# Second graph-attention layer: stored sums, residual rows and small statistics moved to GpSimd, and an eighth closed in nine pieces, one per step

## The chip, the cores and the metric

The kernel runs on one core of a Trainium2 chip. The metric is the device time of one execution in microseconds, the median over several runs. A core has TensorE (PE in the profile; its weight loads are PEld), VectorE (DVE), ScalarE (ACT), GpSimd (POOL) and SyncE (SP), each with a queue of its own that it works off in order, and 16 DMA engines.

## The reference

Two graph-attention layers on the same graph of 4096 nodes, each with a residual and a layer norm:

```python
x = _layernorm(x + gat0(x, adj))   # 8 heads of 128, elu, then a product with W_out and b_out
x = _layernorm(x + gat1(x, adj))   # 4 heads of 64, heads side by side
```

In the second layer, for each head h:

```python
xt  = einsum('ni,hio->hno', x, W)
e   = leaky_relu(src[h, i] + dst[h, j], 0.2), minus infinity where adj[i, j] == 0
att = softmax(e, over j)
out[i, h] = sum over j of att[h, i, j] * xt[h, j]
```

The adjacency has about 32 neighbours a row, and the second layer works on the dense matrix.

## The kernel before, in words

**First layer** (from the start to about 1740 us). It makes lists of neighbours, gathers rows by indirect DMAs from GpSimd's queue (L975) and works through pairs of groups; the second layer's steps are mixed in as their inputs become ready.

**Second layer** (class `Dense`). The target nodes are cut into eight *eighths* of 512 columns, c = 0 to 7, the source nodes into 32 rows of 128, j. A *step* is one (c, j): an adjacency tile `aq` of 512 KB (for two steps) and projected rows `wh` are loaded by SP; ACT makes a mask `mb` of `aq` (L1279, for two steps); DVE makes four weights `e`, one for each head, 128x512 f32, out of `rb` and `mb`, two tiles in SBUF, and a scalar (L1288); PE multiplies them into three PSUM banks `po`, two with the weighted sums (L1312) and one with the denominators (L1322). The functions `load`, `mask`, `weigh` and `multiply` do that, and `ahead` keeps loads four steps, masks two and weights one ahead of the product. There are 14 buffers for `e`, 15 for the sums (pool `sum2`) and two sets of PSUM banks that take turns.

An eighth's steps become ready in *parts*, as the first layer gives rows. When a part that isn't an eighth's last ends, `evict` copies the three banks to SBUF by ACT (L1347) and stores them by ACT's DMA queue in `acc` (L1354). When a later part of the same eighth is to end, its last step's `load` fetches the stored sums back as `hs` (`held` in the code, L1270). PE then adds them into the banks by products with the identity (L1334), and `evict` copies the banks over `hs`.

After the first layer `depth` is 4. There, eighth 4 ends a part (stored once more) at 1898 us, eighth 6 one at about 1974 us, and then the last parts come in the order of c: eighths 0 to 6 with 8, 8, 4, 8, 4, 8 and 4 steps, each ending with stored sums, and eighth 7 with all its 32 steps and none stored.

**Closing of an eighth** (`unit1`). The eighth's last `evict` is followed by 13 pieces on the list `late`: sums of the denominators on PE (`dens`, tile `pd`, L1479), their inversion on DVE (`invert1`, L1488 and L1489), turns of the sums on PE (`turn`, tile `pt`, L1494), scaling on ACT (`share`, L1507), the residual add on DVE (`add`, L1514), means and spreads on ACT with accumulators (L1520, L1530), small 128x4 operations on DVE (`mean` L1524, `spread` L1540, `shift` L1547) and one power on GpSimd (L1541), the norm on ACT and the store of the output by SP (L1556). The order in which the pieces stand between the steps is written out by hand:

```python
while dense.more():
    if dense.weighed:
        dense.multiply()
    dense.ahead()
    late.some(2)
    while dense.ends:
        unit1(*dense.ends.pop(0))
late.all()
```

So after each step two pieces are issued, and every engine meets them in that order between its share of the steps.

Of the kernel before, what the change touches and what calls it, by code (L numbers as in the profile page):

```python
# [15 lines left out]
ALU = mybir.AluOpType  # L16
# [6 lines left out]
EPS = 1e-5  # L23
# [223 lines left out]
class Late:  # L247
# [5 lines left out]
    def add(self, *fs):  # L253
        self.items.extend(fs)
# [37 lines left out]
def fast_path(  # L292
# [11 lines left out]
    nc = tc.nc  # L304
    N, F = x.shape
# [76 lines left out]
    late, then, group, after = Lane(), Lane(), Lane(), Lane()  # L382
# [832 lines left out]
    class Dense:  # L1215
# [78 lines left out]
        def multiply(self):  # L1294
            s, es, wh = self.weighed.pop(0)
            part, j, start, stop = s
            c = part["c"]
            if start:
                self.n += 1
                sets = ((ps_d, "d0", 1), (ps_d, "d1", 1), (ps_d, "d2", 1))  # L1300
                if self.depth > 2 and self.n % 2:
                    sets = ((ps_o, "o0", 2), (ps_o, "o0", 2), (ps_o, "o1", 1))
                part["po"] = [
                    pool.tile([P, HB], F32, tag=tag, name=f"po_1_{c}_{j}_{q}", bufs=b)
                    for q, (pool, tag, b) in enumerate(sets)
                ]
            po = part["po"]
            held = part.get("held") if stop else None
            end = stop and not held
            for q in range(NQ):  # L1310
                for b in range(2 * D1 // DQ):
                    nc.tensor.matmul(  # L1312
                        po[q][ts(b, DQ), :],
                        wh[:, ds(q * 2 * D1 + b * DQ, DQ)],
                        es[2 * q + b * DQ // D1],
                        start=start,
                        stop=end,
                        tile_position=(0, b * DQ),
                        skip_group_check=True,
                    )  # L1320
            for h in range(H1):
                nc.tensor.matmul(  # L1322
                    po[NQ][ts(h, DQ), :],
                    sc1.cj[:, j, h : h + 1].to_broadcast([P, DQ]),
                    es[h],
                    start=start,
                    stop=end,
                    tile_position=(0, h * DQ),
                    skip_group_check=True,
                )  # L1330
            if stop:
                if held:
                    for t, p in zip(held, po):
                        nc.tensor.matmul(  # L1334
                            p, ident, t, start=False, stop=True, skip_group_check=True
                        )
                self.evict(part, held)

        def evict(self, part, hs):
            c = part["c"]  # L1340
            po = part.pop("po")
            hs = hs or [
                self.sum.tile([P, HB], F32, tag="h1", name=f"h_1_{c}_{part['e']}_{q}")
                for q in range(NQ + 1)
            ]
            for t, p in zip(hs, po):
                nc.scalar.copy(t, p)  # L1347
            if part["last"]:
                self.ends.append((c, hs))
                return  # L1350
            if c not in acc_d:
                acc_d[c] = dram.tile([NQ + 1, P, HB], F32, name=f"acc_{c}")
            for k, t in enumerate(hs):
                nc.scalar.dma_start(acc_d[c][k], t)  # L1354
# [114 lines left out]
    def unit1(c, hs):  # L1469
        i0 = c * CQ  # L1470
        rd = small.tile([P, nt, H1], F32, tag="rd", name=f"rd_{c}", bufs=2)
        y_sb = fin.tile([P, nt, F], F32, tag="y", name=f"y_{c}", bufs=6)
        nc.sync.dma_start(y_sb, x1_d[ts(c, HB), :].rearrange("(t p) f -> p t f", p=P))
        held = {}

        def dens():
            pt = held["d"] = ps_m.tile([P, nt, H1], F32, tag="m", name=f"pd_{c}")
            for k in range(nt):
                nc.tensor.matmul(  # L1479
                    pt[:, k],  # L1480
                    hs[NQ][:, ts(k, P)],
                    ident.rearrange("p (m d) -> p m d", d=DQ)[:, :, 0],
                    start=True,
                    stop=True,
                )

        def invert1():
            nc.vector.tensor_scalar(rd, held.pop("d"), NONE, None, ALU.max)  # L1488
            nc.vector.reciprocal(rd, rd)  # L1489

        def turn(q):
            pt = held[q] = ps_m.tile([P, nt, 2, D1], F32, tag="m", name=f"pt_{c}_{q}")
            for k in range(nt):
                nc.tensor.transpose(  # L1494
                    pt[:, k].rearrange("p a d -> p (a d)"), hs[q][:, ts(k, P)], ident
                )

        def share(q, half):
            if half == 0:
                held["z", q] = fin.tile(  # L1500
                    [P, nt, 2, D1], F32, tag="z", name=f"z_{c}_{q}", bufs=2
                )
            z, pt = held["z", q], held[q]
            for k in (2 * half, 2 * half + 1):
                for a in range(2):
                    h = 2 * q + a
                    nc.scalar.activation(  # L1507
                        z[:, k, a], pt[:, k, a], AF.Copy, scale=rd[:, k, h : h + 1]
                    )

        def add(q):
            z = held["z", q].rearrange("p k a d -> p k (a d)")
            y = y_sb[:, :, ts(q, 2 * D1)]
            nc.vector.tensor_tensor(y, y, z, ALU.add)  # L1514

        def means():
            st = held["st"] = small.tile([P, 3, nt], F32, tag="st1", name=f"st_1_{c}", bufs=2)
            for k in range(nt):
                o = fin.tile([P, F], F32, tag="o", name=f"o1_{c}_{k}")
                nc.scalar.activation(o, y_sb[:, k], AF.Copy, accum_out=st[:, 0, k : k + 1])  # L1520

        def mean():
            st = held["st"]
            nc.vector.tensor_scalar(st[:, 0], st[:, 0], -1.0 / F, None, ALU.mult)  # L1524

        def spreads():
            st = held["st"]
            for k in range(nt):
                o = fin.tile([P, F], F32, tag="o", name=f"o2_{c}_{k}")
                nc.scalar.activation(  # L1530
                    o,
                    y_sb[:, k],
                    AF.Square,
                    bias=st[:, 0, k : k + 1],
                    accum_out=st[:, 1, k : k + 1],
                )

        def spread():
            st = held["st"]
            nc.vector.tensor_scalar(st[:, 1], st[:, 1], 1.0 / F, EPS, ALU.mult, ALU.add)  # L1540
            nc.gpsimd.tensor_tensor(  # L1541
                st[:, 1], st[:, 1], neg_half.to_broadcast([P, nt]), ALU.pow
            )

        def shift():
            st = held["st"]
            nc.vector.tensor_tensor(st[:, 2], st[:, 0], st[:, 1], ALU.mult)  # L1547

        def norms():
            st = held["st"]  # L1550
            for k in range(nt):
                y = y_sb[:, k]
                nc.scalar.activation(
                    y, y, AF.Identity, scale=st[:, 1, k : k + 1], bias=st[:, 2, k : k + 1]
                )
            nc.sync.dma_start(out[ts(c, HB), :].rearrange("(t p) f -> p t f", p=P), y_sb)  # L1556

        late.add(
            dens,
            lambda: (invert1(), turn(0)),  # L1560
            lambda: share(0, 0),
            lambda: (share(0, 1), turn(1)),
            lambda: (add(0), share(1, 0)),
            lambda: share(1, 1),
            lambda: add(1),
            means,
            mean,
            spreads,
            spread,
            shift,  # L1570
            norms,
        )

# [16 lines left out]
    with tc.manual_schedule():  # L1590
        verdict()
        while dense.more():
            if dense.weighed:
                dense.multiply()
            dense.ahead()
            late.some(2)
            while dense.ends:
                unit1(*dense.ends.pop(0))
        late.all()
# [3 lines left out]
def kernel(  # L1603
# [21 lines left out]
    with ExitStack() as inner:  # L1625
        fast_path(
            inner, tc, flag_sb, x, xT, adj, adjT, w0f, w0T, a0, w_out, b_out, w1f, w1T, a1, out
        )
# [48 lines left out]
```

## Time and profile before

| | us |
|---|---|
| median of 9 runs (lowest to highest) | 2240.29 (2232.39 to 2245.64) |
| profiled execution, its own time | 2245.11 |
| its span | 2243.3 |
| PE busy (its share of the span) | 1624.5 (72%) |
| DVE busy | 1537.1 (69%) |
| POOL busy | 1173.3 (52%) |
| ACT busy | 813.8 (36%) |
| granted TensorE clock, mean | 0.877 |

The costs of operations in the stage from 1995 to 2132 us, by groups: an `e` 745 ns (consecutive ones overlap), an identity product 610 ns for each of its two passes, a copy of a bank 585 ns, a residual add on DVE 687 ns, a small 128x4 operation on DVE 162 to 169 ns, the power on POOL 1166 ns. PE's ends are modelled, so its busy share is not read as work; distances between starts are.

In the views below a line of a timeline has the start in us, the length in us, the engine, the line of the kernel, the operation, output and inputs by name, the number of instructions, and in brackets how long the engine had been idle before it and what ended that.

### The profile page before, as it was taken

The page shows a single profiled execution, that of the slowest core. Times are in us where ns is not written, and L with a number is a line of the kernel's source. Part 1 is how long each engine was busy: PE and PEld are TensorE (multiplying, and loading weights), DVE is VectorE, ACT ScalarE, POOL GpSimd, SP SyncE. Part 2 cuts the span into 40 slices and gives each one's busy share as a digit, 9 for nine tenths or more (in the row PEclk, how much of TensorE's full clock was granted, in tenths as well). Part 3 has the DMA queues.
Part 4 walks back from the last instruction along what each step waited for, and adds up shares of the span by engine and source line. Part 5 has one row for each costly group of instructions (what it writes and reads, how often), then busy time and mean ns, then how long its engine had stood idle before and what let it go on. Part 6 is the DMA issues. An engine that isn't in the chain of part 4 may idle for free. (4 is left out here: it accounts for less than half of the span.)

```text
span 2243.3 us, 34216 instructions
## 1 busy us (share of the span) xinstructions
PE 1624.5 (72%) x12092; PEld 845.2 (38%) x12092; DVE 1537.1 (69%) x3456; ACT 813.8 (36%) x1811; POOL 1173.3 (52%) x1189
## 2 busy tenths in 40 slices
PE   3414455556666753787599778788899989999996
PEld 2412333344343432544334334434444433333332
DVE  1533657646837836677687984978677677997896
ACT  3143433434434433434334424222233313235552
POOL 0056767777777777677677756766776000000000
PEclk9999667777887877697799988989999999999998
DMA  6888977857968957977878986655676337566651
GB/s 183 142 291 142 226 153 214 161 160 213 236 159 262 209 154 210 203 216 206 241 196 286 246 164 205 216 168 174 229 250 218 108 118 250 175 207 244 232 173 40
DMA packets 202259, 442.11 MB, mean 197 GB/s; under 512 B 52643, under 2 KB 76310, under 8 KB 199134
## 3 DMA queue, kind: packets, MB, share of 16 engines
q1 hardware_dynamic: 123790, 261.44, 36.5%
q0 software_dynamic: 55296, 161.10, 31.1%
q10 hardware_dynamic: 22992, 17.29, 2.4%
q8 instruction: 98, 1.61, 0.3%
q14 instruction: 83, 0.68, 0.1%
HBM read 414.81 MB, written 29.08 MB: 198 GB/s over the span
## 5 line engine op out<-in xcount | busy, mean ns | idle before, releaser
L975 POOL DMA_INDIRECT G<-table,ids x1152 | 1160.8, 1008 | 563.2 <-issue 301.7
L1288 DVE SCALAR_TENSOR_TENSOR e<-rb,pj,mb 128x512 f32<-128x512 f32 x1024 | 697.3, 749 | 116.3 <-PE po L1322 69.3
L1312 PE MATMUL po<-e,wh 128*32 128x512 f32 x4096 | 606.6, 628 | 98.5 <-DVE e L1288 98.5
L1322 PE MATMUL po<-e,cj 128*32 128x512 f32 x2048 | 344.1, 607 | 0.0
L1020 ACT ACTIVATE ag<-po,void 128x257 f32<-128x257 f32 x288 | 120.8, 471 | 528.2 <-PE pa L1037 503.5
L1312 PEld LDWEIGHTS po<-e,wh 128*32 128x32 f32 x4096 | 158.8, 112 | 395.7 <-DVE e L1288 237.8
L1069 PE MATMUL ph<-aT,w_sb 128*128 128x128 f32 x1152 | 185.3, 328 | 161.8 <-DVE hT L1083 151.4
L1541 POOL TENSOR_TENSOR st<-st,neg_half 128x4 f32<-128x4 f32 x8 | 9.2, 1152 | 495.6 <-DVE st L1540 495.6
L994 DVE TENSOR_TENSOR e<-rb,G 128x256 f32<-128x256 f32 x144 | 61.0, 423 | 281.8 <-DMA G<-table,ids 275.5
L1069 PEld LDWEIGHTS ph<-aT,w_sb 128*128 128x128 f32 x1152 | 174.8, 240 | 184.6 <-issue 111.9
L1010 PE MATMUL po<-G,e 128*32 128x257 f32 x2304 | 192.9, 450 | 63.8 <-DVE e L1001 28.5
L647 ACT ACTIVATE mb<-aq,less 114x1024 fp8e4<-114x1024 int32 x144 | 165.9, 1153 | 84.5 <-DMA aq<-in_adj 78.4
L1279 ACT ACTIVATE mb<-aq 128x1024 bf16<-128x1024 int32 x128 | 134.7, 1057 | 148.2 <-DVE e L1288 78.9
L1322 PEld LDWEIGHTS po<-e,cj 128*32 128x32 f32 x2048 | 97.1, 114 | 135.0 <-issue 110.9
L1090 PE MATMUL py<-wo_sb,hT 128*128 128x256 f32 x576 | 138.3, 396 | 5.6 <-DVE hT L1083 5.6
L1010 PEld LDWEIGHTS po<-G,e 128*32 128x32 f32 x2304 | 77.8, 123 | 132.1 <-issue 58.9
L1090 PEld LDWEIGHTS py<-wo_sb,hT 128*128 128x128 f32 x576 | 113.2, 202 | 22.5 <-DVE hT L1083 6.8
L1037 PE MATMUL pa<-ident,ag 128*128 128x128 f32 x576 | 109.5, 320 | 15.4 <-DVE pc L461 8.3
L1037 PEld LDWEIGHTS pa<-ident,ag 128*128 128x128 f32 x576 | 70.7, 159 | 114.1 <-issue 74.2
L1028 DVE TENSOR_TENSOR ag<-ag,rd_all 128x512 f32<-128x512 f32 x144 | 100.7, 699 | 8.9
L1039 ACT COPY aT<-pa 128x512 f32<-128x512 f32 x144 | 84.9, 589 | 18.8 <-DVE key L659 8.4
L1083 DVE SCALAR_TENSOR_TENSOR hT<-el,ph 128x512 f32<-128x512 f32 x72 | 48.2, 670 | 57.9 <-ACT el L1080 57.8
(182 smaller groups left out, 1590.3 us busy)
## 6 DMA issues: line engine op xcount, KB each, us to landing
aq<-in_adj SPq DMA_DIRECT2D x140, 512.0 KB
aq<-in_adjT SPq DMA_DIRECT2D x128, 512.0 KB
wh<-wh_d SPq DMA_DIRECT2D x128, 256.0 KB
rb<-r_d SPq DMA_DIRECT2D x23, 1024.0 KB
rb<-r_d SPq DMA_DIRECT2D x36, 512.0 KB
G<-table,ids POOLq DMA_INDIRECT x1152
hs<-acc SPq DMA_DIRECT2D x45, 256.0 KB
acc<-hs ACTq DMA_DIRECT2D x24, 256.0 KB
```

The source lines that it names most:

```text
L647: nc.scalar.activation(bins[m], raw.pop(m)[0:R], AF.Sign, bias=less[0:R], accum_out=held["deg"][:, t, q : q + 1], saturate=False,)
L975: nc.gpsimd.indirect_dma_start(out=G[:, b, :], out_offset=None, in_=table[:, :], in_offset=bass.IndirectOffsetOnAxis(ap=lists[s][0][:, c : ...
L1010: nc.tensor.matmul(po[ts(b, H0 * T), :], e[:, m * NB + b].rearrange("p h t -> p (h t)"), G[:, m * NB + b, 0 : F + 1], start=True, stop=Tru ...
L1020: nc.scalar.activation(ag[:, m], po, AF.Identity, bias=void[:, 0, v : v + 1])
L1028: nc.vector.tensor_tensor(ag[:, :, 0:F], ag[:, :, 0:F], rd.unsqueeze(2).to_broadcast([P, 2, F]), ALU.mult)
L1037: nc.tensor.transpose(pt[:, c, m], ag[:, m, ts(c, P)], ident)
L1069: nc.tensor.matmul(phs[k][:, hh, :], w_sb[:, c, ts(h, D0)], aT[:, c, h, :], start=(c == 0), stop=(c == KC - 1),)
L1090: nc.tensor.matmul(pys[0], hT[:, h, :], wo_sb[:, h, :], start=(h == 0), stop=(h == H0 - 1))
L1279: nc.scalar.activation(self.mb, aq, AF.Relu, scale=OPEN)
L1288: nc.vector.scalar_tensor_tensor(e, part["rb"][:, h], sc1.pj[:, j, h : h + 1], mb, ALU.max, ALU.min)
L1312: nc.tensor.matmul(po[q][ts(b, DQ), :], wh[:, ds(q * 2 * D1 + b * DQ, DQ)], es[2 * q + b * DQ // D1], start=start, stop=end, tile_position ...
L1322: nc.tensor.matmul(po[NQ][ts(h, DQ), :], sc1.cj[:, j, h : h + 1].to_broadcast([P, DQ]), es[h], start=start, stop=end, tile_position=(0, h ...
```

## The change

- In the stage after the first layer (`depth` above 2) stored sums are no longer added by PE. ACT copies the banks to three new tiles, and GpSimd adds `hs` to each. In the earlier stage PE still adds them.
- The three copies are made in reverse order everywhere, the denominators' first.
- The residual adds, `mean`, the first operation of `spread`, and `shift` go from DVE to GpSimd.
- The 13 pieces become nine: the denominators' sums with the first turn, the inversion by itself, the two halves of each scaling together, mean with spreads, spread with shift. One piece is issued per step, two while the list is longer than nine.

```diff
@@ multiply
-            end = stop and not held
+            end = stop and (not held or self.depth > 2)
...
             if stop:
-                if held:
+                if not end:
                     for t, p in zip(held, po):
                         nc.tensor.matmul(
                             p, ident, t, start=False, stop=True, skip_group_check=True
                         )
-                self.evict(part, held)
-
-        def evict(self, part, hs):
+                self.evict(part, held, end)
+
+        def evict(self, part, held, apart):
             c = part["c"]
             po = part.pop("po")
-            hs = hs or [
+            hs = held if held and not apart else [
                 self.sum.tile([P, HB], F32, tag="h1", name=f"h_1_{c}_{part['e']}_{q}")
                 for q in range(NQ + 1)
             ]
-            for t, p in zip(hs, po):
+            for t, p in zip(hs[::-1], po[::-1]):
                 nc.scalar.copy(t, p)
+            if held and apart:
+                for t, u in zip(hs[::-1], held[::-1]):
+                    nc.gpsimd.tensor_tensor(t, t, u, ALU.add)
@@ unit1: add, mean, spread, shift
-            nc.vector.tensor_tensor(y, y, z, ALU.add)
+            nc.gpsimd.tensor_tensor(y, y, z, ALU.add)
...
-            nc.vector.tensor_scalar(st[:, 0], st[:, 0], -1.0 / F, None, ALU.mult)
+            nc.gpsimd.tensor_scalar(st[:, 0], st[:, 0], -1.0 / F, None, ALU.mult)
...
-            nc.vector.tensor_scalar(st[:, 1], st[:, 1], 1.0 / F, EPS, ALU.mult, ALU.add)
+            nc.gpsimd.tensor_scalar(st[:, 1], st[:, 1], 1.0 / F, EPS, ALU.mult, ALU.add)
...
-            nc.vector.tensor_tensor(st[:, 2], st[:, 0], st[:, 1], ALU.mult)
+            nc.gpsimd.tensor_tensor(st[:, 2], st[:, 0], st[:, 1], ALU.mult)
@@ the pieces
-            dens,
-            lambda: (invert1(), turn(0)),
-            lambda: share(0, 0),
-            lambda: (share(0, 1), turn(1)),
-            lambda: (add(0), share(1, 0)),
-            lambda: share(1, 1),
+            lambda: (dens(), turn(0)),
+            invert1,
+            lambda: (share(0, 0), share(0, 1), turn(1)),
+            lambda: (add(0), share(1, 0), share(1, 1)),
             lambda: add(1),
             means,
-            mean,
-            spreads,
-            spread,
-            shift,
+            lambda: (mean(), spreads()),
+            lambda: (spread(), shift()),
             norms,
@@ the loop
-            late.some(2)
+            late.some(2 if len(late.items) > 9 else 1)
```

In the built program 24 products leave PE's queue, and GpSimd's gets 24 adds of stored sums, 16 residual adds and 24 small operations. In this queue the adds of an eighth's sums can stand ahead of the small operations of the eighth before it.

## The prediction

> **What bounds the kernel now.** I read the page's slices first, to find the stage that the change touches.
>
> ```profile
> PE   3414455556666753787599778788899989999996
> DVE  1533657646837836677687984978677677997896
> POOL 0056767777777777677677756766776000000000
> ```
>
> A slice is 56.1 us. POOL is empty from slice 32 (1740 us) on: the gathers are over and only second-layer steps run. Next I cut that stage in windows; the columns behind the window are its length and the busy time of PE, PEld, DVE, ACT and POOL.
>
> ```profile
> 1903.00:1998.00 95.00, 95.00 (x850) 37.13 (x842) 94.76 (x144) 20.67 (x23) 0.00 (x0) 1.00 0.63 210
> 1998.00:2165.00 167.00, 163.73 (x1283) 58.18 (x1284) 134.80 (x233) 96.71 (x291) 8.21 (x7) 1.00 0.59 204
> 2165.00:2220.00 55.00, 55.00 (x502) 22.67 (x498) 53.90 (x83) 11.96 (x14) 0.00 (x0) 1.00 0.36 121
> ```
>
> In the first and third window no eighth is closed and DVE never rests; in the middle one, where seven eighths end and are closed, it rests or does other things for a fifth of the time. So I took DVE's timeline there, around the closing of eighth 0.
>
> ```profile
> 1903.24 95.51 DVE L1288 SCALAR_TENSOR_TENSOR e<-rb,pj,mb 128x512 f32<-128x512 f32 x144 [0.41 <-ACT mb L1279]
> 2001.92 0.17 DVE L1488 TENSOR_SCALAR rd<-pd 128x16 f32<-128x16 f32 x1 [3.17 <-PE pd L1479]
> 2002.13 0.25 DVE L1489 RECIPROCAL rd<-rd 128x16 f32<-128x16 f32 x1
> 2002.30 5.30 DVE L1288 SCALAR_TENSOR_TENSOR e<-rb,pj,mb 128x512 f32<-128x512 f32 x8
> 2007.52 0.69 DVE L1514 TENSOR_TENSOR y<-y,z 128x512 f32<-128x512 f32 x1
> ...
> 2016.74 0.17 DVE L1540 TENSOR_SCALAR st<-st 128x4 f32<-128x4 f32 x1
> 2018.07 0.16 DVE L1547 TENSOR_TENSOR st<-st 128x4 f32<-128x4 f32 x1 [1.17 <-POOL st L1541]
> ```
>
> A weight e costs 95.51/144 = 0.663 us, a step (four) 2.65 us, and nothing on DVE comes between them except the closing, which DVE does in line and for which it waits (the brackets). Last, PE's timeline at the same place.
>
> ```profile
> 1995.35 2.84 PE L1334 MATMUL po<-hs,ident 128*128 128x512 f32 x6
> 1998.12 1.93 PE L1312 MATMUL po<-e,wh 128*32 128x512 f32 x16
> 2000.83 1.05 PE L1479 MATMUL pd<-ident,hs 128*128 128x4 f32 x8
> 2001.75 0.63 PE L1494 MATMUL pt<-ident,hs 128*128 128x128 f32 x4
> ```
>
> The identity products hold PE 2.77 us (1995.35 to 1998.12). An unhindered step takes 2.57 us (in the chain ten steps reach from 1903.42 to 1929.16, 2.574 each). Two steps with the sums and both turns of an eighth reach from 1998.12 to 2005.61, 7.49 us, so these cost 7.49 - 5.15 = 2.34 us.
>
> Two sums over the rest. **DVE**, from the last e of the 144 (1998.75) to the last e of all (2218.9): 220.1 us, of which 264 e make 175.0, waits 31.9 (the brackets added up) and closing work 13.2. **PE**, from 1995.35 to 2220.6, 225.3 us: 68 steps make 175.0, seven closings 16.4, seven identity products 19.4, together 210.8; it stands about 14. DVE is the bound, PE is close behind.
>
> **Removed.** In this stretch, 21 identity products leave PE (19.4 us), and 14 residual adds and 21 small operations leave DVE. What stays on DVE is the inversion of the denominators, 7 x (0.17 + 0.25) = 3.0 us. Its wait goes too: sums and turn now come a step before it, so PE has a whole step (2.57) to produce pd, where DVE waited 3.17 or 0.26. The waits on ACT and POOL leave DVE because POOL does those operations. DVE would then need 175.0 + 3.0 = 178.0 us, PE 210.8 - 19.4 = 191.4: if nothing else happened PE would be late next.
>
> **Added.** POOL gets, in this stretch, 21 adds of stored sums and 14 of residual rows, all 128x512 f32 with two inputs in SBUF. No such POOL row exists. The nearest is the 128x128 f32 select that builds the identity, 282 ns; a 128x1 memset takes 95, so 512 elements cost 95 + 4 x 187 = 843 ns with one input. With a second input read after the first it is 95 + 8 x 187 = 1.59 us. I take 1.0 us, closer to the row than to its double, because write and loop are paid once.
>
> Does an add disturb the e's? Two rows of the same POOL operation answer half of it, with the DVE row that ran beside the second:
>
> ```profile
> 2016.99 1.05 POOL L1541 TENSOR_TENSOR st<-st,neg_half 128x4 f32<-128x4 f32 x1 [289.06 <-DVE st L1540]
> 2071.94 1.38 POOL L1541 TENSOR_TENSOR st<-st,neg_half 128x4 f32<-128x4 f32 x1 [23.57 <-DVE st L1540]
> 2071.71 2.74 DVE L1288 SCALAR_TENSOR_TENSOR e<-rb,pj,mb 128x512 f32<-128x512 f32 x4
> ```
>
> At 2016.99 DVE was idle, waiting for the result: 1.05 us. At 2071.94 an e had begun 0.23 us earlier: 1.38 us, and so in all three cases with e's running. The extra 0.35 us reaches to 0.6 us after the e's start, that is, to its end. POOL does not get its operands while an e reads. The e's lost nothing then, but POOL's four columns fit between two of them. I take it that it holds the other way round: while POOL reads 512 columns, no e proceeds. So each add costs DVE b = 1.0 us, from 0 (if e's have precedence) to 1.59. 35 x 1.0 = 35.0 us, and DVE needs 178.0 + 35.0 = 213.0 against 220.1: **-7.1 us**. PE (191.4) stays behind DVE's pace, so its new waits, the turn of eighths 0 and 1 that stands behind three adds, are covered by 21.6 us of slack; without that cover each costs up to 2.4 us.
>
> The rule that speaks against the change is in the Trainium skill, SBUF — State Buffer, section "Who interferes with whom": a VectorE instruction with two SBUF inputs contends with a GpSimd instruction that reads SBUF, and the one that comes second stands still until the first is done. An e has two (rb and mb). It agrees with 1.38 against 1.05, and goes further than the rows, which show no e delayed. GPSIMD Engine Reference, section "Elementwise — side-by-side cycle accounting", has 2.6 cycles per element for two inputs; an estimate from it is 512 x 2.6 / 1.2 GHz = 1.11 us per add, and the sum by it would be 1.8 us over the time before, not 2.1 under.
>
> **Eighth 4's earlier end (1898 us)** is treated alike, but its sums go to memory by ACT, whose three issues (1.3 us) now wait for POOL, and three masks are queued behind them on ACT. Before: copies to 1901.3, issues, first mask done 1903.2, e's resume 1903.24. After: PE is done 2.77 us sooner, copies end at 1899.5, three adds of 1.0, each behind an e's 0.6, end near 1903.2; issues, mask, e's at 1905.6: **+2.4 us** (0.8 if POOL need not wait, 4 with 1.59).
>
> **The end.** Eighth 7 stores nothing first, so only its closing counts; DVE is idle and b does not apply. The first residual add hides under the second half's scaling (2224.97 to 2226.6); the second is bare, 1.0 for 0.69: +0.3. Mean, spread and shift each lose a hop and pay POOL's start (0.09 for the memset, 1.05 for the power): at 0.3 us each, +0.3 altogether. Copying in reverse lets the sums start as before and the first turn 0.1 later. **+0.6 us** (-0.5 to +3).
>
> **Costed at nothing.** The reversed copies in the first layer's stage: a next part is loaded only when nothing is loaded or masked, so at least a mask (1.06) and an e (0.75) stand between; uncovered it is two copies (1.2 us) for each of 13 ends. The 15 sum buffers, now six per eighth instead of three: the fifth set back was released eight steps or more before it is needed; without that SP stalls, and the masks' loads behind it. The output store moves on SP behind the next two loads, with the next mask's load after it; the mask is due some five steps later. ACT, which was late 5.59, 4.68 and 2.83 us in the waits, gets the small statistics' answers from a POOL queue that may hold three adds; the masks behind them have 2 to 3 steps of cover. I charge **+2 us** for this, 13.1 at most.
>
> Sum: -7.1 + 2.4 + 0.6 + 2.0 = -2.1 us. The profiled execution took 2245.1 us (span 2243.3), 4.8 over the median; applied to the median 2240.3 it is **2238.2 us**. In general the change is -37.1 + 35 b, with zero at b = 1.06.
>
> **Rivals.** (1) *POOL does not hold up DVE* (b near 0). For it: no e was delayed beside a power. Against it: the 0.35 us. Then PE's 191.4 decides: from 1995.35 it ends at 2186.8 instead of 2220.6, -33.8; with 0.8 for eighth 4, 0.6 at the end, 0.5 for turns and half of ACT's 13.1, -25: 2215 us. (2) *Slower: the adds take DVE's place.* One mechanism, each POOL add stopping the e's for longer than the work and waits that left DVE; it decides from b = 1.06. At 1.3, half way between my value and the doubled row, it is +8.4, 2248.7 us; at 1.59, +18.6, 2258.9. For it: two inputs, and a handover each way that no row prices. Against: 31.9 us of waits is a lot to make up. (3) *The waits do not go*: ACT stays late as before (13.1 us instead of 2.0), 2249.3 us; I count it with (2).
>
> **Chances.** A change smaller than 0.2% (4.5 us) can't be told from none here. The forecast's case, b from 0.85 to 1.15, 0.36: of it 0.10 faster, 0.22 the same, 0.04 slower; its own range is 2230 to 2244. Rival 1, with what lies between, 0.28. Rivals 2 and 3, 0.36. So faster 0.38, same 0.22, slower 0.40. The range, 2214 to 2256, reaches from rival 1 into rival 2 short of its far end.
>
> **What would show it.** Right: no L1334 after 1740 us; the e's 0.66 us apart except where a POOL add runs, and there a gap of about 1 us; DVE's brackets on ACT, POOL and pd gone; PE waiting for e's. Rival 1: adds beside undisturbed e's, PE steps 2.57 apart, DVE waiting for e buffers. Rival 2: POOL adds over 1.1 us each with an equal gap between e's. I am wrong altogether if the time is under 2214, or if the last e ends on time and the end after it has grown by over 3 us.

## The result, and the profile after

The changed kernel takes **2270.24 us** (median of 15 runs, 2252.32 to 2277.55) against 2237.1 us for the kernel before beside it (46 runs): ratio 1.014, 95% interval 1.0122 to 1.0158. It is 33 us slower; forecast were 2238.2 us in a range of 2214 to 2256. Its profiled execution took 2275.55 us with a span of 2273.7, 30.4 more than before.

The slices of the page (56.8 us each here):

```profile
PE   3424555456677555696688868888998989988896
DVE  1533666546848636687778967877776768988795
POOL 0066777777777677677677747757773000034640
```

POOL is now busy in slices 36 to 39, where it was empty, and DVE has not come nearer to nine tenths there. The windows that answer to the three of before, set at the same places of the work:

```profile
1908.00:2003.00 95.00, 92.35 (x808) 36.27 (x806) 91.28 (x135) 20.16 (x21) 2.56 (x2) 1.00 0.58 193
2005.00:2194.00 189.00, 164.55 (x1282) 55.89 (x1276) 149.75 (x207) 93.18 (x285) 104.34 (x60) 0.94 0.56 192
2194.00:2249.00 55.00, 54.04 (x480) 24.71 (x480) 53.10 (x80) 13.34 (x22) 2.61 (x3) 0.97 0.33 106
```

DVE has fewer instructions in the middle window than before (207 for 233) and is busy longer (149.75 us for 134.80). POOL is busy for 104.34 us with 60 instructions.

To place the 30.4 us I cut the spans at steps counted from the end:

| us | before | after | |
|---|---|---|---|
| first layer, to its last projection | 1879.7 | 1886.5 | +6.8 |
| from there to eighth 6's first weight | 17.8 | 16.1 | -1.7 |
| eighth 6's first 28 steps and eighth 0's 8 ("the 36 steps") | 95.9 | 102.4 | +6.5 |
| eighth 1's first weight to eighth 7's 13th step ("the 48 steps") | 172.5 | 189.1 | +16.6 |
| eighth 7's last 20 steps | 52.3 | 52.3 | 0.0 |
| last weight to the end | 25.2 | 27.2 | +2.0 |

The 48 steps lost most. DVE's time there, from the distances between the starts of its instructions:

| us | before | after |
|---|---|---|
| weights e, undisturbed | 127.5 | 127.8 |
| e's held up beside a POOL instruction | 0 | 19.4 (22 e's) |
| DVE idle | 32.2 | 39.4 |
| closing work on DVE | 12.8 | 2.5 |

The closing work left DVE as planned. The idle time did not leave; it grew: DVE now waits 32.0 us there for masks, 5.9 for added denominators and 1.3 for PE's products. (PE's granted clock is 0.94 in the middle window for 1.00 before; by the 1.3 us a slower PE is no main cause.) DVE's timeline at the closing of eighth 0, and further on:

```profile
1989.13 23.95 DVE L1288 SCALAR_TENSOR_TENSOR e<-rb,pj,mb 128x512 f32<-128x512 f32 x36 [1.79 <-ACT mb L1279]
2015.85 0.17 DVE L1491 TENSOR_SCALAR rd<-pd 128x16 f32<-128x16 f32 x1 [2.77 <-PE pd L1482]
...
2055.46 9.80 DVE L1288 SCALAR_TENSOR_TENSOR e<-rb,pj,mb 128x512 f32<-128x512 f32 x8 [0.62 <-ACT mb L1279]
...
2129.56 12.00 DVE L1288 SCALAR_TENSOR_TENSOR e<-rb,pj,mb 128x512 f32<-128x512 f32 x18
2151.49 2.74 DVE L1288 SCALAR_TENSOR_TENSOR e<-rb,pj,mb 128x512 f32<-128x512 f32 x4 [9.92 <-ACT mb L1279]
```

POOL's timeline at the same places, and at the end of the kernel:

```profile
2007.80 8.84 POOL L1350 TENSOR_TENSOR h<-h,hs 128x512 f32<-128x512 f32 x3 [97.23 <-ACT h L1347]
...
2053.57 5.78 POOL L1350 TENSOR_TENSOR h<-h,hs 128x512 f32<-128x512 f32 x3 [7.22 <-ACT h L1347]
2059.32 3.40 POOL L1517 TENSOR_TENSOR y<-y,z 128x512 f32<-128x512 f32 x2
...
2133.66 11.46 POOL L1350 TENSOR_TENSOR h<-h,hs 128x512 f32<-128x512 f32 x3 [5.23 <-ACT h L1347]
2145.09 1.26 POOL L1517 TENSOR_TENSOR y<-y,z 128x512 f32<-128x512 f32 x1
...
2253.40 1.26 POOL L1517 TENSOR_TENSOR y<-y,z 128x512 f32<-128x512 f32 x1 [54.46 <-ACT z L1510]
```

An add takes 1.26 us alone (last line, DVE idle). Beside e's there are two regimes.

*Turns.* From 2055.46 eight e's take 9.80 us instead of 5.4, beside POOL's adds: four e's in a row start 1.68 us apart instead of 0.663. Add and e alternate, and each add costs 1.02 us of DVE.

*Standing still.* From 1989.13 36 e's take 23.95 us, 0.663 each, undisturbed until 2013.08. POOL's first add began at 2007.80 and ended at 2014.19, 6.39 us later, 1.1 us after the last e. In the 48 steps five of 35 adds stood like that, for 6.4, 2.4, 9.0, 9.0 and 10.9 us. Three others that also began amid undisturbed e's got in after the e in progress and took 1.28 to 1.55 us.

What stands behind such an add is on PE's timeline and on ACT's.

```profile
2014.25 1.57 PE L1482 MATMUL pd<-ident,h 128*128 128x4 f32 x8 [4.51 <-POOL h L1350]
```

```profile
2133.00 1.57 ACT L1347 COPY h<-po 128x512 f32<-128x512 f32 x3 [4.29 <-PE po L1322]
2134.43 1.08 ACT L1279 ACTIVATE mb<-aq 128x1024 bf16<-128x1024 int32 x1
2146.38 0.42 ACT L1523 ACTIVATE o<-y 128x256 f32<-128x256 f32 x1 [10.86 <-POOL y L1517]
...
2150.41 1.04 ACT L1279 ACTIVATE mb<-aq 128x1024 bf16<-128x1024 int32 x1
```

At 2133.66 an add of stored sums begins and gets nothing until DVE's 18 e's are done (2141.56). Behind it in POOL's queue stands the residual add of the eighth before (2145.09); on that ACT's mean waits 10.86 us; behind the mean in ACT's queue stands the next mask; and DVE waits 9.92 us for this mask. The add came through at 2142.68, 1.1 us after DVE had run out of masks. So here DVE shuts the add out, and the add, by way of ACT, starves DVE.

### The profile page after: what moved, and what is told of

Its sections match the earlier page's. It is cut to its first block, busy times and chain, and to the rows that moved or that the text cites. A ratio compares the mean times of both kernels' runs of the same rounds, so it can differ in the third digit from the quotient of the medians.

```text
span 2273.7 us, 34194 instructions
## 1 busy us (share of the span) xinstructions
PE 1622.6 (71%) x12044; PEld 844.9 (37%) x12044; DVE 1548.4 (68%) x3416; ACT 809.0 (36%) x1811; POOL 1281.2 (56%) x1253
## 5 line engine op out<-in xcount | busy, mean ns | idle before, releaser
L1288 DVE SCALAR_TENSOR_TENSOR e<-rb,pj,mb 128x512 f32<-128x512 f32 x1024 | 718.1, 769 | 159.1 <-ACT mb L1279 81.9
L1312 PE MATMUL po<-e,wh 128*32 128x512 f32 x4096 | 629.9, 634 | 110.1 <-DVE e L1288 108.0
L1322 PE MATMUL po<-e,cj 128*32 128x512 f32 x2048 | 354.8, 609 | 0.0
L1010 PE MATMUL po<-G,e 128*32 128x257 f32 x2304 | 192.0, 449 | 59.6 <-DVE e L1001 27.8
L1350 POOL TENSOR_TENSOR h<-h,hs 128x512 f32<-128x512 f32 x24 | 55.8, 2349 | 306.2 <-DVE e L1288 176.2
L1028 DVE TENSOR_TENSOR ag<-ag,rd_all 128x512 f32<-128x512 f32 x144 | 100.5, 698 | 8.9
L724 ACT ACTIVATE ws<-pw,base 128x512 uint8<-128x512 f32 x72 | 48.0, 689 | 103.6 <-PE pw L714 99.6
```

The lines of the kernel that those rows point to most:

```text
L1010: nc.tensor.matmul(po[ts(b, H0 * T), :], e[:, m * NB + b].rearrange("p h t -> p (h t)"), G[:, m * NB + b, 0 : F + 1], start=True, stop=Tru ...
L1028: nc.vector.tensor_tensor(ag[:, :, 0:F], ag[:, :, 0:F], rd.unsqueeze(2).to_broadcast([P, 2, F]), ALU.mult)
L1288: nc.vector.scalar_tensor_tensor(e, part["rb"][:, h], sc1.pj[:, j, h : h + 1], mb, ALU.max, ALU.min)
L1312: nc.tensor.matmul(po[q][ts(b, DQ), :], wh[:, ds(q * 2 * D1 + b * DQ, DQ)], es[2 * q + b * DQ // D1], start=start, stop=end, tile_position ...
L1322: nc.tensor.matmul(po[NQ][ts(h, DQ), :], sc1.cj[:, j, h : h + 1].to_broadcast([P, DQ]), es[h], start=start, stop=end, tile_position=(0, h ...
```

## The experiments

All stretches below are those of the two tables. The first eight kernels ran on two chips where the first layer takes some 245 us longer (the kernel before has medians of 2488 and 2482 us there), the last three on one like that of the result; ratios are to the kernel before on the same chip, while the times in us that are expected for a whole kernel are those of the result's chip. The stretches of the second layer hardly depend on the chip: a kernel that left the work of the 48 steps and of the 36 unchanged had 172.5 us there too, and 97.4 for 95.9. Each stretch comes from one profile.

**1. One part of the change at a time.** Three kernels: only the stored sums back on PE,

```diff
-            end = stop and (not held or self.depth > 2)
+            end = stop and not held
```

> The changed kernel, with the stored sums added by TensorE with the identity again (residual rows and small statistics stay on GpSimd, nine pieces stay). Theory 1, GpSimd's adds and VectorE's weights exclude each other at SBUF, so that adds stand still while weights follow each other without a pause, and TensorE, ScalarE and with them the masks wait for the adds: 24 of the 40 long adds go, the waits of the sums (pd) for them too; about 2245 to 2258 us, with residual adds that still take over 1.26 us each beside weights. Theory 2, the order in nine pieces, one per step, is what costs: as the changed kernel, 2265 to 2272. Theory 3, GpSimd is only slow (1.26 us an add where nothing disturbs it) and its queue in order: about 2250, with adds of 1.26 us throughout.

only the residual rows and small statistics back on DVE,

```diff
-            nc.gpsimd.tensor_tensor(y, y, z, ALU.add)
+            nc.vector.tensor_tensor(y, y, z, ALU.add)
... (mean, spread and shift likewise)
```

> The changed kernel, with residual rows and small statistics on VectorE again (stored sums stay on GpSimd, nine pieces stay). Theory 1: the sums' adds are still held up by the weights (2.3 us each on average), TensorE's sums and turns wait for them, but ScalarE waits less: 2248 to 2262 us. Theory 2: 2265 to 2272. Theory 3: about 2250, adds of 1.26 us throughout.

and both, so that the nine pieces and the reversed copies are left.

> Only the order in nine pieces, one per step, and the reversed copies: stored sums by TensorE, residual rows and small statistics on VectorE, as before the change. Theory 1: no adds on GpSimd, and VectorE's waits of before (31.9 us) mostly go, so that TensorE's 210.8 us bound the stretch of 220: 2225 to 2235 us, under the kernel before. Theory 2: 2260 or more. Theory 3 says the same as theory 1.

| | ratio | 36 steps | 48 steps | of it idle | e's held | end |
|---|---|---|---|---|---|---|
| before | 1 | 95.9 | 172.5 | 32.2 | 0 | 25.2 |
| changed | 1.014 (1.0122 to 1.0158) | 102.4 | 189.1 | 39.4 | 19.4 | 27.2 |
| sums on PE | 1.0069 (1.0032 to 1.0106) | 100.0 | 173.1 | 30.9 | 12.4 | 27.1 |
| rows on DVE | 1.0108 (1.0057 to 1.0159) | 101.9 | 180.1 | 26.6 | 11.3 | 25.4 |
| pieces and reversed copies | 1.0069 (1.0031 to 1.0107) | 100.4 | 178.3 | 37.7 | 0 | 25.3 |

The third kernel has no add on GpSimd and loses all the same, which none of the three theories had (two put it below the kernel before, one at 2260 us or more). On its base the rows alone gain 5.2 us in the 48 steps, the sums alone lose 1.8, and both together lose 10.8: the parts don't add up. That fits one queue in which the rows of one eighth stand behind the sums of the next, as at 2133.66. The end belongs to the rows and statistics (27.1 and 27.2 against 25.2 to 25.4).

**2. Adds for which nobody waits.** The kernel before, with an add of the same size on GpSimd for each of eighth 7's late steps, into a tile that nothing reads, released by a one-column copy of the step's mask.

```diff
+            if c7 and 8 <= j7 < 28 and not late.items:
+                t = 31 - j7
+                nc.scalar.copy(tick[:, t : t + 1], dense.mb[:, 0, 0:1])
+                nc.gpsimd.tensor_tensor(side[:, 0], side[:, 1], tick[:, t : t + HB], ALU.add)
```

> The kernel before, with up to 20 additional GpSimd adds 128x512 f32 on tiles of their own beside the steps of eighth 7 (released one per step by a one-column copy on ScalarE), whose results nobody reads. Theory 1, and the first to start keeps the other out: the weights stay 0.663 us apart for long stretches, the adds take many us each, and the time is that of before within 0.3%. The prediction's reckoning, each add takes 1.0 to 1.26 us from the weights: 13 to 20 adds, 13 to 25 us more. Theory 3: adds of 1.26 us, weights undisturbed, time as before.

DVE's timeline and POOL's there:

```profile
2412.42 53.09 DVE L1288 SCALAR_TENSOR_TENSOR e<-rb,pj,mb 128x512 f32<-128x512 f32 x80
```

```profile
2415.86 71.58 POOL L1605 TENSOR_TENSOR side<-side,tick 128x512 f32<-128x512 f32 x17 [4.55 <-ACT tick L1604]
2487.39 1.02 POOL L1541 TENSOR_TENSOR st<-st,neg_half 128x4 f32<-128x4 f32 x1
```

Eighty e's ran at 0.664 us each as if there were no POOL. The first of the 17 adds stood still for 50.78 us, from 2415.86 to 1.1 us past the last e; the other 16 then took 1.09 to 1.66 us each. The e's lost nothing, the 48 steps are 172.5 us as before, and of the loss (ratio 1.006, 1.0029 to 1.0092, some 15 us) 9.1 us are in the end: 34.3 us for 25.2, because the closing's power stands behind the adds (second line). While these e's followed each other without a pause, the add did not run more slowly; it did not run. That is one add, the others queued behind it; in the changed kernel some do get in between two e's.

**3. GpSimd instructions that read nothing.** The changed kernel with two memsets of the same tile in place of each 128x512 add. Stored sums and residual rows are left out of the result. The queues stay, and so do the waits but for one: a memset doesn't wait for the scaled rows, for which the residual adds of the changed kernel waited 25.6 us on POOL.

```diff
-                    nc.gpsimd.tensor_tensor(t, t, u, ALU.add)
+                    nc.gpsimd.memset(t, 1.0)
+                    nc.gpsimd.memset(t, 1.0)
... (the residual add likewise)
```

> The changed kernel with each GpSimd add 128x512 replaced by two fills of the same tile, which only write (stored sums and residual rows are left out of the result, and with the residual add the wait for the scaled sums). Theory 1, adds and weights exclude each other because both read SBUF: fills take 0.4 to 0.7 us each beside running weights, none stands still, the weights stay 0.663 us apart, and the stretch from eighth 1's first weight to eighth 7's 13th step takes 160 to 172 us instead of 189. Rival, anything on GpSimd beside the weights does it: fills stretched to many us or weights stretched by them, 180 us or more.

Groups of POOL in the stage of the closings:

```profile
L1529 POOL TENSOR_SCALAR st<-st 128x4 f32<-128x4 f32 x7 | 37.1, 5297 | 24.6 <-ACT o L1525 24.6
L1350 POOL MEMSET h<- 128x512 f32 x21 | 11.1, 526 | 135.7 <-ACT h L1347 135.7
```

All 70 memsets took 0.53 us, beside e's or not, and no e was held. The 48 steps fell to 158.0 us. What is left on GpSimd that reads SBUF is tiny, and it still stands: the seven means, 128x4, took 0.25 us where DVE paused and 5.3 on average, one of them 10.03. POOL's line of this one, then DVE's beside it:

```profile
2249.42 10.03 POOL L1529 TENSOR_SCALAR st<-st 128x4 f32<-128x4 f32 x1 [8.89 <-ACT o L1525]
```

```profile
2240.81 18.55 DVE L1288 SCALAR_TENSOR_TENSOR e<-rb,pj,mb 128x512 f32<-128x512 f32 x28
```

It ended 0.1 us after DVE's 28 e's had. ACT waited 25.8 us for these means, and 27.6 of DVE's 27.8 us of idle are waits for masks, which stand behind them in ACT's queue. So what is contended for is reading, and how long an instruction is shut out doesn't go by its size. Nor does a slow GpSimd explain the loss: two memsets fill its queue for 1.05 us, where an add alone takes 1.26. The 36 steps (100.2 us) and eighth 7's last 20 (55.6) stay longer than in the kernel before, and the whole ratio, 1.0022 (0.9991 to 1.0054), doesn't separate this kernel from that one.

The Trainium skill, SBUF — State Buffer, section "Who interferes with whom", states this lock: a VectorE instruction with two SBUF inputs contends with a GpSimd instruction that reads SBUF, not with one that only writes. The 50.78 us, the 0.53 us and the 10.03 us agree. The 50.78 us go further: there the add had to wait not for one VectorE instruction but for all that were left of 80 in a row.

**4. The reversed copies alone,** on the kernel before.

```diff
-            for t, p in zip(hs, po):
+            for t, p in zip(hs[::-1], po[::-1]):
```

> The kernel before with nothing but the three copies of a part in reverse order. Theory 1, the first copy now waits for the bank that is finished last, so that ScalarE frees itself, and with it the next mask, 1 to 2 us later at each of the 23 ends of parts: the stretch of eighth 6's part and eighth 0 (36 steps) goes from 96 us to 100 to 102, and the whole kernel is 0.2 to 0.6% slower. Rival, the copies' order is free (the prediction's zero): 96 to 97 us there, and a ratio within 0.2% of one.

Ratio 1.0092 (1.0055 to 1.013), where 1.002 to 1.006 was expected: this one line, costed at nothing, loses about two thirds of what the whole change loses. The 36 steps take 100.5 us (+4.6), the 48 steps 178.3 (+5.8). ACT's timeline at one eighth's end, first in the kernel before,

```profile
2039.50 0.58 ACT L1347 COPY hs<-po 128x512 f32<-128x512 f32 x1 [4.60 <-PE po L1334]
2040.36 0.58 ACT L1347 COPY hs<-po 128x512 f32<-128x512 f32 x1 [0.27 <-PE po L1334]
2041.21 0.59 ACT L1347 COPY hs<-po 128x512 f32<-128x512 f32 x1 [0.27 <-PE po L1334]
```

then in this kernel:

```profile
2286.99 1.56 ACT L1347 COPY hs<-po 128x512 f32<-128x512 f32 x3 [6.31 <-PE po L1334]
```

PE finishes the banks in forward order, 0.86 us apart, and ACT copied each while PE worked on the next. In reverse the first copy waits for the last bank, and the other two (0.98 us, 1.56 less 0.58) come behind it. Masks and means stand behind the copies on ACT, and DVE waits for the means: at this place its wait grew from 2.83 us to 3.81. Six ends lie in the 48 steps; 6 x 0.98 = 5.9, and 5.8 was measured. Of the 4.6 us in the 36 steps, 3.6 lie at eighth 4's end: its stores and three masks stand behind the copies there, and DVE waited 4.04 us for a mask where it had waited 0.41.

**5. The change with forward copies, and the nine pieces alone with forward copies.**

```diff
-            for t, p in zip(hs[::-1], po[::-1]):
+            for t, p in zip(hs, po):
```

> The changed kernel with the three copies of an eighth's sums made in forward order again; the adds on GpSimd and the nine pieces stay. Theory (three mechanisms that add up: the reversed copies make the masks late, the adds hold up the weights, and PE, ACT and then the masks queue behind the adds): the reversed copies' share goes, which the reversed copies alone showed as 4.6 us in the 36 steps of eighths 6 and 0 and 5.8 us in the 48 steps of eighths 1 to 7, so 102.4 becomes about 98 and 189.1 about 183; the ratio to the kernel before falls from 1.014 to about 1.010. Rival (the masks are late behind the adds anyway, so the order of the copies doesn't matter): 102 and 189 stay, the ratio stays at 1.014.

> The kernel before with nothing changed but the closing in nine pieces, one per step: sums on PE, additions and statistics on DVE, copies in forward order. Theory (nine pieces neither help nor harm, since each eighth's closing still waits for ACT and POOL in line on DVE): 96 us for the 36 steps and 172.5, give or take 3, for the 48, ratio 1.000 +- 0.002. Rival A (the pieces themselves made the 5.8 us that the pieces with reversed copies showed): 178 in the 48 steps, ratio about 1.003. Rival B (they do what the prediction wanted, a step between question and answer): below 165, ratio under 0.997.

| | ratio | 36 steps | 48 steps | of it idle | e's held |
|---|---|---|---|---|---|
| changed, forward copies | 1.0051 (1.0026 to 1.0076) | 99.2 | 179.2 | 22.8 | 26.6 (28 e's) |
| nine pieces, forward copies | 1.0019 (0.9995 to 1.0043) | 96.4 | 173.4 | 32.8 | 0 |

With the copies forward the change loses 0.5% instead of 1.4%. That is more back than expected (1.010, and 183 us in the 48 steps), and more, some 20 us, than the 13.1 us of the two stretches. Of 35 adds two stand still instead of five, and more of them take turns with e's. The nine pieces by themselves leave DVE's idle time where it was (32.8 for 32.2): their effect is not told from none.

**6. Another way to take the waits off DVE.** First the kernel before with only the order of closing changed: 14 slots, one taken per step by every eighth that is open, so that two closings run beside each other and there are one or two steps between question and answer.

```diff
+        for pieces in closers:
+            pieces.pop(0)()
... (the list of 14 slots in place of the 13 pieces)
```

> The kernel before with another order of the closing alone: 14 slots, one per step, for every eighth that is open (so that two eighths are closed beside each other), with VectorE's and ScalarE's pieces two steps apart where one waits for the other; all work on the engines of before. Theory: what is left of VectorE's waits (33 us in that stretch, in the kernel before as in the nine pieces alone) comes from pieces that follow each other too closely across engines; it falls to under 15 us and the stretch from 172.5 to 158 to 166 us, TensorE then being the bound; ratio 0.994 to 0.998. Rival, the waits are TensorE's own length (bound 211 of 220 us): ratio within 0.2% of one.

Then the same, and in an eighth's last part DVE adds the stored sums straight out of PSUM, two steps after the end; the identity products and ACT's copies of these parts are gone.

```diff
+            for t, p in zip(hs[::-1], po[::-1]):
+                nc.vector.tensor_tensor(t, p, t, ALU.add)
... (no identity products and no copies in such a part)
```

> The kernel of the run with closings beside each other, and the stored sums of an eighth's last part added by VectorE straight out of the banks (one input in PSUM, one in SBUF, 128x512) instead of TensorE's identity products and ScalarE's copies, in a slot of their own two steps after the part's end. Theory: TensorE loses 19 us and VectorE gains 21 x 0.7 = 15 us in the stretch, so VectorE (127 of weights, 13 of closing, 15 of sums) bounds it at about 155 to 162 us; ratio 0.990 to 0.996. Rival, VectorE waits for the banks in line: 168 us or more.

> The version with 14 slots that close open eighths beside each other and with the stored sums added by DVE straight out of PSUM, once more, for a narrower interval. It gave 0.9857 [0.978, 0.9935] and 151.5 us in the 48 steps. Theory (DVE's waits are gone there, 0.2 us idle): 0.990 within 0.004, 95 to 96 us and 151 to 153 us. Rival (that ratio was a lucky draw of the first layer, which scatters by 1%): above 0.995 while the 48 steps still take 152 us.

| | ratio | 36 steps | 48 steps | of it idle | closing on DVE |
|---|---|---|---|---|---|
| closings beside each other | 0.9972 (0.9938 to 1.0007) | 96.3 | 160.7 | 21.3 | 12.5 |
| and sums out of PSUM | 0.9857 (0.978 to 0.9935) | 95.7 | 151.5 | 0.2 | 24.6 |
| the same, again | 0.9905 (0.9876 to 0.9933) | 96.0 | 151.5 | 0.2 | 24.6 |

The first of the two brings the 48 steps down by 11.8 us, with 21.3 us of idle left where under 15 was expected; its ratio is not told from one. The second is faster than the kernel before, 2207.53 us against 2228.75 in its second run, and so than the changed one. Of the 21.2 us the 48 steps give 21.0 (172.5 less 151.5). What PE's relief and what the missing copies give by themselves was not separated. DVE's timeline and its window in that run:

```profile
1975.18 1.87 DVE L1566 TENSOR_TENSOR hs<-po,hs 128x512 f32<-128x512 f32 x3
1976.97 8.02 DVE L1288 SCALAR_TENSOR_TENSOR e<-rb,pj,mb 128x512 f32<-128x512 f32 x12
1984.92 0.15 DVE L1491 TENSOR_SCALAR rd<-pd 128x16 f32<-128x16 f32 x1
```

```profile
1967.20:2118.70 151.50, 151.50 (x1270) 59.95 (x1264) 151.26 (x260) 81.59 (x260) 6.46 (x6) 1.00 0.68 238
```

No bracket is left: DVE never waits (busy 151.26 of 151.50 us). Three sums cost DVE 1.79 us up to the next e; it took work on, twice the closing it had, and won, because what it had been losing was waits (32.2 us, now 0.2).

## Why the prediction was wrong

**The price of an add was right, where it applied.** It was put at b = 1.0 us of DVE per add, from 0 to 1.59. Adds and e's that take turns show 1.02 (1.683 apart, less 0.663). That it came so near is luck in part: it was taken as the add's own length, which alone is 1.26, and of which not all falls on DVE. But 22 e's were held, for 19.4 us, where the sum had 35.0. The step "while POOL reads 512 columns, no e proceeds" was taken for all 35 adds, and only in that direction. The trace of before had shown the other direction, the power that waited for the e to end, and I read it as a delay of one e at most. It has no such bound: an add that is shut out stands as long as e's follow each other, 50.78 us in the experiment.

**The step that failed first: "the waits on ACT and POOL leave DVE because POOL does those operations".** The sum took 31.9 us of waits off DVE and gave 2.0 back for ACT's lateness. In the 48 steps DVE's idle time went from 32.2 to 39.4 us. These 39.4 us for 2.0 are what the sum missed: with the 19.4 for 35.0 of held e's they turn its -5.1 us (-7.1 and 2.0) into the +16.6 measured, to within 0.2 us. The operation left DVE's queue, but what it waits for and who waits for it stayed: DVE still needs the masks, these stand behind the means and spreads on ACT, and those now wait for a POOL queue in which an add can be shut out by DVE. ACT's waits on POOL there are 62.4 us (30.5 for rows, 20.5 and 11.4 for statistics). The line "ACT ... gets the small statistics' answers from a POOL queue that may hold three adds" named the mechanism and priced it at 2 us with a cover of 2 to 3 steps (5 to 8 us); three of the five adds that stood took 9 to 11.

**The term costed at nothing: the reversed copies.** I looked for their cost only in the first layer, with a mask and an e as cover, and bounded it there by 1.2 us for each of 13 ends. In the stage of the closings nothing was charged for them (0.1 us for a turn at the very end). Alone on the kernel before they cost 0.98 us for each end there, since ACT's queue had no slack: DVE's waits on ACT (5.59, 4.68, 2.83 us) were in the trace, and a delay of ACT adds to them. In the whole kernel they make 0.9% (some 23 us on the chip that they ran on).

**PE.** It does the stage without the sums and is no bound, as said; its 21.6 us of slack did not have to carry only "the turn behind three adds": PE waited 10.9 us for added denominators at its matmuls in three places, and DVE's inversion behind it twice, 5.9 us. So a step between question and answer didn't suffice there either.

**Eighth 4's end** was put at +2.4 us, 4 at most. Eighth 6's 28 steps, in which it lies, took 79.3 us for 74.7, +4.6: 20 e's beside the three adds took 16.57 us instead of 13.3, and DVE then waited 1.93 us for the mask behind the stores. The path that was forecast, the masks behind stores that wait for POOL, is there, but it isn't shown to be the cause: the reversed copies alone, without any add, make it 78.3 us, and the adds with forward copies 78.0.

**The end** was put at +0.6 and is +2.0. Up to the last norm it is +0.9: the first add hides, as said, the second costs 1.26 for 0.69, the hops at the mean add 0.1, and those from the spread to the norm together another 0.1. The other 1.1 us lies behind the last norm, with the store: 8.3 to 8.5 us in the kernels that have rows and statistics on DVE, 9.3 to 9.5 in those that have them on GpSimd. Why was not settled.

**The rivals.** Rival 1 (b near 0) is ruled out where adds take turns; where e's do have precedence, it cost time instead of saving it. Rival 2 had the sign, but not by its mechanism, an add dearer than 1.06 us. Rival 3, ACT stays late, is what happened to the waits; I bounded it at 2249.3 by ACT's old waits, and never asked how long an add could stand. The forecast treated the three as alternatives, and the chip did two at once.

**What stays open.** The first layer's +6.8 us: three kernels with the same instructions up to there had 1853.5 to 1871.7 us on one chip, so one profile settles nothing. There is an indirect sign that the reversed copies cost there too. Take the loss of each kernel by its ratio, and subtract what its profile loses from eighth 6's first weight on: what is left for the time before is 6 to 13 us in each of the six kernels with reversed copies, and from -14 to 4 in the six with forward ones. That would be 0.5 to 1.0 us for each of the 13 ends, under the 1.2 by which they were bounded; it is an estimate from medians, and no trace shows it.

And what decides between turns and standing still was not settled. In the five profiles with adds on GpSimd, 35 adds began amid e's that were 0.663 apart, with no add just before them. Of these 24 got in after the e in progress or the next, and 11 stood. All 11 had begun 0.10 to 0.26 us after the start of an e; of the 16 that began 0.33 us or more after it none stood. But eight that got in had begun as early as those that stood, 0.06 to 0.17 us after the start. So the moment of arrival matters and doesn't decide alone.

## What to carry to other kernels

Before an operation goes to an idle engine, ask not only what it costs there but whether it can run at all beside what the busy engine streams, and follow the wait round: if the busy engine's next input stands behind the answer, the two shut each other out. A wait leaves an engine only when its answer comes in time, not when the waiting instruction is moved; spreading question and answer over steps, and adding straight out of PSUM so that copies, products and hops disappear, took all of it away with more work on the busiest engine. The order of a few copies is not free: read which producer finishes first and who queues behind the last copy.

## What the runs showed of the hardware that was not expected

- A GpSimd 128x512 add with two SBUF inputs stood still for 50.78 us beside 80 VectorE instructions of two SBUF inputs in a row, which lost nothing (0.664 us each). Even a 128x4 operation stood 10.03 us.
- Most of the adds that begin amid such e's get in between two of them (24 of 35). Where both take turns, the add takes 1.72 us and the VectorE instruction 1.76 instead of 0.745; starts are 1.68 apart.
- GpSimd memsets of 128x512 f32 take 0.53 us beside the same VectorE stream.
- VectorE's add with one input in PSUM (three in 1.87 us) costs no more than that with both in SBUF (means of 0.677 and 0.681 us in the last run).
